# Attention over 400,000 sorted edges: 138 dense groups in place of 136, lookups five to a batch, counts five, four and then three, and later nodes counted in one block

## The chip, the cores and the metric

The kernel runs on one NeuronCore of a Trainium2 chip. Its engines are TensorE (PE, with its weight loads as PEld), VectorE (DVE), ScalarE (ACT), GpSimd (POOL) and SyncE (SP). The metric is the device time of one launch in microseconds (us); less is better. Before the change three runs gave 3430.93, 3432.67 and 3432.46 us, a median of 3432.46 us.

## The reference

One graph-attention layer with a residual and a layer norm. There are 12,500 nodes with 64 features, 400,000 edges with 64 features of their own, and the edges are sorted by destination:

```python
h_src = nfeats[src]; h_dst = nfeats[dst]
e = leaky_relu(concat([h_src, h_dst, efeats]) @ W_attn + b_attn, 0.01)[:, 0]
m = concat([h_src, efeats]) @ W_ne
alpha = exp(e - segment_max(e, dst)[dst]); alpha /= segment_sum(alpha, dst)[dst]
z = segment_sum(alpha[:, None] * m, dst)
out = relu(concat([nfeats, z]) @ W_out)
x = layernorm(x + out, eps=1e-5)
```

Destinations are drawn as 12500·u², so the first nodes have very many edges and the last ones few.

## The kernel before, in words

**Groups.** The edges are cut into 782 groups of 512 (128 partitions times T = 4). A group covers a window of neighbouring destination nodes: a few nodes at the start of the list, up to 48 at its end.

**Sparse groups and batches.** Groups 136 to 781 are done by gathering: for each group POOL issues four indirect DMAs (`gather`, L335), each of which fetches 128 rows of a table in HBM into a tile `zx`; SP fetches the edges' own rows into the same tile. A tile holds four groups, and there are ZB = 9 of them. Groups go in 42 batches of 16 (four tiles each); the last four batches have 10, 10, 12 and 6. For one batch DVE makes `scores` tile by tile (L370 to L388), then `softmax` (L669 on, starting with the transpose at L694) runs in five steps over partitions and lines with four small DMA round trips by ACT, then `weights` (L791), and PE multiplies weights by gathered rows (`products`, L808). Two of a batch's four tiles are multiplied at once, the other two (`later`) between the softmax steps of the next batch; only then is a `zx` tile free for a new gather. DVE adds the sums into a ring (`add_in`, L827).

**Dense groups.** The first 136 groups have so few nodes that nothing is gathered for them. *Lookups* find the source's score: ACT turns a row of source numbers into a 0/1 matrix (`look_turn`, L427 and L428, a buffer of the pool `big`), PE multiplies (L438), DVE picks (`look_scores`, L463 to L469), and `look_rows` (L448 to L457) adds the edges' own part for a whole batch. When all groups of a *round* (`ROUNDS`) are looked up, they take part in the softmax of the next batch that is free for it. *Counts* then sum the weights by source and node: for each of four columns ACT writes a 0/1 block (L477, L478, a `big` buffer each), DVE writes `lows` (L480), PE multiplies the two into a PSUM bank (L485), and DVE adds the bank into `counts` (`dense_sum`, L503). A block of 490 columns covers five nodes. For a sixth, seventh or eighth node there is one more `big` buffer each, with four Square operations of 98 columns (L490), one Relu (L491), four matmuls (L493) and one addition (L506).

**Chunks.** Groups whose nodes lie together form a chunk (`CHUNKS`). In the batch after a chunk's last count PE multiplies `counts` by all node features (`node_products`, L562, 50 records), DVE picks the result and clears `counts` (`node_pick`, L570 to L575). `edge_products` (L546) does the edges' part once per batch.

**The order.** All of this is one hand-written order: a Python loop emits, batch by batch and tile by tile, the instructions of every engine, and each engine runs its list in order. At the second tile of the next batch stand: its lookup (L427), the blocks of count 0 (L477), and then `between` (`far`, L635, and four more by ACT; `step`, L639, by DVE). At the third tile stand `look_rows` and count 1, at the fourth `ep` is loaded. In the softmax's steps stand counts 2 and 3 and the lookups after the second one. `dense_step` sums open counts in steps 0 and 3. The number of `big` buffers is BIG = 6.

**What a batch has.** `alike` takes up to four groups for the lookups of a batch and up to four for its counts, and stops at the ends of rounds, of node limits (`NODS`) and, for counts, of chunks. That gives lookups in batches 1 to 34, four each, and counts in batches 5 to 38, four each:

| counts per group | batches, before |
|---|---|
| 2 nodes | 5 to 8 |
| 3 nodes | 9 to 13 |
| 4 nodes | 14 to 19 |
| 5 nodes | 20 to 26 |
| 6 nodes | 27 to 31 |
| 7 nodes | 32 to 36 |
| 8 nodes | 37 and 38 |

A chunk ends in batches 13, 16, 19, 21, 23, 25 and in each of 26 to 38.

Of the kernel before, what the change touches and what calls it, by code (L numbers as in the profile page):

```python
# [9 lines left out]
F32 = mybir.dt.float32  # L10
# [5 lines left out]
P = 128  # L16
T = 4
# [10 lines left out]
BIG = 6  # L28
# [30 lines left out]
def sorted_path(ctx, tc, x, dst, idx, edge, w_ne, w_attn, b_attn, w_out, out, flag):  # L59
# [24 lines left out]
    ones_row = const.tile([1, P], F32, name="ones_row")  # L84
    nc.vector.memset(ones_row, 1.0)
# [3 lines left out]
    ENDS = ((3, 3, 2, 2), (3, 3, 2, 2), (3, 3, 3, 3), (2, 2, 1, 1))  # L89
# [25 lines left out]
    def each_of(g):  # L115
        return next(n for upto, n in EACHS if g < upto)

# [105 lines left out]
    sixth, seventh, eighth, probe = cut(pps, NB, NB, NB, 8)  # L223
    more_nodes, w_dst, w_src = (sixth, seventh, eighth), sixth[:, 0:D], seventh[:, 0:D]
# [18 lines left out]
    def dense_places(srcs, fit):  # L243

        assert max(n for _, n in NODS) <= FIT + len(more_nodes)
# [43 lines left out]
    def slots_of(k):  # L289

        g0, G = starts[k], sizes[k]
        drel = chunks.tile([P, T, BG], F32, name="drel", bufs=3)
# [69 lines left out]
    def scores(g0, n, zx, drel, b0, plain):  # L362
# [6 lines left out]
        pr = feats.tile([P, SG, T, D], F32, name="pr", bufs=1)  # L369
# [37 lines left out]
    def look_loads(g0, n):  # L407

        many = nodes_of(g0)
        wrow = tiny.tile([P, EACH, NOD], F32, name="wrow_d", bufs=1)[:, :, 0:many]  # L410
        nc.sync.dma_start(out=wrow[:, 0:n], in_=wins[g0 // P][g0 % P:g0 % P + n, 0:many].unsqueeze(0).to_broadcast([P, n, many]))
        return dense_edges(g0, n, "ed", True), wrow
# [28 lines left out]
    def look_rows(g0, n, loads):  # L441
# [4 lines left out]
        pr = feats.tile([P, SG, T, D], F32, name="pr", bufs=1)  # L446
# [12 lines left out]
    def look_scores(g, found):  # L459

        pr = feats.tile([P, SG, T, D], F32, name="pr", bufs=1)
# [9 lines left out]
    def dense_counts(g):  # L471
# [14 lines left out]
        for j in range(nodes_of(g) - FIT):  # L486
            at = wide + j * NB
            hi = big().rearrange("l p t -> l (p t)")[:, 0:T * NB].rearrange("l (t h) -> l t h", t=T)
            for t in range(T):
                nc.scalar.activation(hi[:, t], places[:, at:at + NB], AF.Square, bias=place[:, t, g:g + 1])  # L490
            nc.scalar.activation(hi, hi, AF.Relu, scale=-1.0, bias=1.0)  # L491
            for t in range(T):
                nc.tensor.matmul(more_nodes[j], lows[t], hi[:, t], start=(t == 0), stop=(t == T - 1), skip_group_check=True)  # L493
        return g, to

    def dense_sum(g, to):
# [69 lines left out]
    def node_pick(g0, pairs):  # L566

        pr = feats.tile([P, SG, T, D], F32, name="pr", bufs=1)
# [62 lines left out]
    def between(k):  # L631
# [17 lines left out]
    def at_ends(step, same, pen, mask):  # L649
# [6 lines left out]
    def lines_of(step, same, pen, mask):  # L656
# [4 lines left out]
        return step, same, pen, mask, rw  # L661

    def softmax(k, about, carry, d=None, carry_d=None):
# [8 lines left out]
        step, same, pen, mask = about[0:4]  # L672
# [29 lines left out]
        to_lines(ends_of, bnd)  # L702
        yield
        in_lines()
        rw = about[4]
# [173 lines left out]
    with before:  # L879
# [23 lines left out]
        with tc.manual_schedule(engines={EngineType.DVE, EngineType.Pool, EngineType.Activation, EngineType.PE, EngineType.SP}):  # L903
# [27 lines left out]
            nc.vector.tensor_copy(edge_both, pwt[:, 2, 0:D])  # L931
            d0f = pre.tile([1, NG], F32, name="d0f", bufs=1)
# [131 lines left out]
    def centred(c0, po):  # L1064
# [15 lines left out]
        sq = feats.tile([P, SG, T, D], F32, name="pr", bufs=1)[:, 0]  # L1080
# [6 lines left out]
    def scaled(c0, yo, sq, var, more=False):  # L1087
# [3 lines left out]
        if more:  # L1091
            nc.scalar.activation(scrap_row[:, 0:1], ones_row[:, 0:1], AF.Exp)
# [23 lines left out]
    with loop:  # L1116
# [38 lines left out]
        def alike(todo, ends_=chunk_ends):  # L1155
# [676 lines left out]
```

## Time and profile before

The profiled execution took 3432.35 us; its span, from the first to the last instruction, is 3430.6 us.

| engine | busy us | share of the span | instructions |
|---|---|---|---|
| PE | 2334.8 | 68% | 10444 |
| DVE | 2232.5 | 65% | 5723 |
| ACT | 1382.4 | 40% | 3178 |
| POOL | 2454.1 | 72% | 2614 |

How to read it: no engine is busy all the time, and the shares are means over a kernel whose stages differ. A useful mark is the transpose at L694, which DVE does once per batch, when all scores of the batch are there. In this document *stretch k* runs from that mark of batch k to that of batch k+1. It holds the softmax and the weights of batch k, the scores of batch k+1, the softmax-time lookups and counts of batch k, and the first lookups and counts of batch k+1. Stretch 26 begins 2186.8 us after the span's start, stretch 37 at 3145.8, stretch 41 at 3391.2.

### The profile page before, as it was taken

The numbers are of one execution on the slowest core, as the hardware profiler recorded it, in microseconds if no ns is written. First come the engines' busy times: TensorE is split into PE (matmuls) and PEld (weight loads), VectorE is DVE, ScalarE is ACT, GpSimd is POOL, SyncE is SP. The second block draws the span as 40 slices with busy tenths as digits, with TensorE's granted clock in tenths as the row PEclk, the third lists the DMA queues.
The fourth block names the chain that finished last, engine by engine and source line by source line (L and its number), as shares of the span: only waits on it lengthen the run. The fifth ranks groups of instructions, "written<-read, shape, count | busy, mean of one in ns | idle before, by whom it ended". The sixth has DMA issues, their size and how long they took to land. (4 is left out here: it accounts for less than half of the span.)

```text
span 3430.6 us, 40536 instructions
## 1 busy us (share of the span) xinstructions
PE 2334.8 (68%) x10444; PEld 1953.5 (57%) x10444; DVE 2232.5 (65%) x5723; ACT 1382.4 (40%) x3178; POOL 2454.1 (72%) x2614
## 2 busy tenths in 40 slices
PE   0244445666667676765777787788888788888864
PEld 0244445565566565664666565666666666666653
DVE  5654455666666667666676767767777667675565
ACT  0111123433333434344344544445554555565632
POOL 6777777777777777777777777777777776774460
PEclk9999996555555566666666676677777777777865
DMA  9433334334444434343343434344344333332230
GB/s 128 88 67 67 66 73 76 75 74 79 84 77 80 89 63 94 74 76 76 75 79 74 76 76 91 76 77 77 74 80 76 67 71 74 63 65 53 43 68 11
DMA packets 821663, 253.18 MB, mean 74 GB/s; under 512 B 740890, under 2 KB 780009, under 8 KB 821426
## 3 DMA queue, kind: packets, MB, share of 16 engines
q1 hardware_dynamic: 697356, 163.64, 24.2%
q0 software_dynamic: 82912, 86.20, 14.7%
q10 hardware_dynamic: 41158, 0.66, 0.7%
q8 instruction: 90, 1.47, 0.2%
q14 instruction: 147, 1.20, 0.1%
HBM read 243.18 MB, written 6.80 MB: 73 GB/s over the span
## 5 line engine op out<-in xcount | busy, mean ns | idle before, releaser
L335 POOL DMA_INDIRECT zx<-table,srcs x2520 | 2383.5, 946 | 869.8 <-issue 702.3
L808 PE MATMUL pg<-w,zx 128*128 128x40 f32 (+9 forms) x5024 | 983.0, 366 | 165.4 <-DMA zx<-table,srcs 99.5
L808 PEld LDWEIGHTS pg<-w,zx 128*128 128x128 f32 x5024 | 962.7, 297 | 182.7 <-issue 99.6
L485 PE MATMUL pg<-big,lows 128*128 128x490 f32 (+3 forms) x1088 | 582.9, 700 | 381.2 <-DVE lows L480 325.4
L485 PEld LDWEIGHTS pg<-big,lows 128*128 128x128 f32 x1088 | 282.7, 274 | 623.6 <-issue 430.1
L438 PE MATMUL pg<-s_src,big 128*128 128x98 f32 x1088 | 291.3, 445 | 302.0 <-DVE pr L465 162.9
L438 PEld LDWEIGHTS pg<-s_src,big 128*128 128x128 f32 x1088 | 266.1, 328 | 305.3 <-issue 171.7
L477 ACT ACTIVATE big<-places,place 128x490 f32<-128x490 int16 (+3 forms) x544 | 338.5, 622 | 80.0 <-PE pg L438 56.1
L478 ACT ACTIVATE big<-big 128x490 f32<-128x490 f32 (+3 forms) x544 | 296.3, 545 | 17.3
L372 DVE TENSOR_REDUCE fixed<-pr 128x16 f32<-128x1024 f32 (+2 forms) x168 | 199.3, 1186 | 155.6 <-ACT fixed L368 146.4
L377 DVE TENSOR_TENSOR fixed<-fixed,zx 128x16 f32<-128x16 f32 (+2 forms) x168 | 30.9, 184 | 360.5 <-DMA zx<-table,srcs 356.4
L562 PE MATMUL pg<-xall,counts 128*128 128x256 f32 x950 | 243.1, 421 | 3.5 <-DVE yo L1079 3.3
L562 PEld LDWEIGHTS pg<-xall,counts 128*128 128x128 f32 x950 | 201.0, 215 | 42.7 <-issue 9.8
L370 DVE TENSOR_TENSOR pr<-zx,lines 128x1024 f32<-128x1024 f32 (+2 forms) x168 | 197.0, 1173 | 4.8 <-DMA zx<-in_edge_dram 4.4
L368 ACT ACTIVATE fixed<-wrow 128x80 f32<-128x80 f32 (+9 forms) x168 | 44.6, 265 | 354.8 <-DVE lows L480 130.1
L480 DVE TENSOR_SCALAR lows<-fixed,low,kept 128x128 f32<-128x128 f32 x544 | 185.3, 401 | 2.5 <-PE pg L485 2.5
L696 ACT ACTIVATE soft<-turned 128x128 f32<-128x128 f32 x42 | 16.3, 389 | 414.0 <-DVE turned L694 414.0
L427 ACT ACTIVATE big<-low_of,p_col 128x512 f32<-128x512 bf16 x136 | 98.0, 720 | 186.6 <-DMA low_of<-low_rows 141.6
L827 DVE TENSOR_TENSOR acc<-acc,pg 128x28 f32 (+9 forms) x646 | 120.2, 186 | 69.2 <-issue 21.9
L490 ACT ACTIVATE big<-places,place 128x98 f32<-128x98 int16 x336 | 97.7, 362 | 70.3 <-PE pg L438 52.5
L803 PE MATMUL pg<-zx,ident 1*1 1x32 f32 (+2 forms) x336 | 41.2, 207 | 123.5 <-issue 115.1
L379 DVE TENSOR_TENSOR hot<-fixed,drel 128x320 bf16<-128x320 f32 (+9 forms) x168 | 107.8, 642 | 6.0 <-issue 0.2
(400 smaller groups left out, 2703.0 us busy)
## 6 DMA issues: line engine op xcount, KB each, us to landing
zx<-in_edge_dram SPq DMA_DIRECT2D x645, 128.0 KB
zx<-table,srcs POOLq DMA_INDIRECT x2520
ed<-in_edge_dram SPq DMA_DIRECT2D x34, 512.0 KB
low_of<-low_rows SPq DMA_DIRECT2D x136, 128.0 KB
ep<-in_edge_dram SPq DMA_DIRECT2D x136, 128.0 KB
table<-xall SPq DMA_DIRECT2D x7, 455.0 KB
out_dram<-yo SPq DMA_DIRECT2D x24, 128.0 KB
xall<-in_x_dram SPq DMA_DIRECT2D x13, 224.0 KB
```

Source lines behind the costliest of these rows:

```text
L335: nc.gpsimd.indirect_dma_start(out=zx[0:r, g, t, 1:EW] if plain else zx[0:r, g, t, 0:EW], out_offset=None, in_=x[:, :] if plain else table ...
L370: nc.vector.tensor_tensor(pr[0:r, 0:n], ze[0:r, 0:n], w_edge[0:r].unsqueeze(1).to_broadcast([r, n, T, D]), op=OP.mult)
L372: nc.vector.tensor_reduce(ysum[0:r, 0:n], pr[0:r, 0:n], axis=AX.X, op=OP.add)
L379: nc.vector.tensor_tensor(hot[0:r, 0:n], slots[0:r, 0:Sk].unsqueeze(1).unsqueeze(1).to_broadcast([r, n, T, Sk]), drel[0:r, :, b:b + n].rea ...
L438: nc.tensor.matmul(found[:, t, :], hot[:, :, t], s_src, start=True, stop=True)
L477: nc.scalar.activation(hi, places[:, 0:wide], AF.Square, bias=place[:, t, g:g + 1])
L478: nc.scalar.activation(hi, hi, AF.Relu, scale=-1.0, bias=1.0)
L480: nc.vector.tensor_scalar(lows[t], count_, low[:, t, g:g + 1], kept[:, t, kept_at(g):kept_at(g) + 1], op0=OP.is_equal, op1=OP.mult)
L485: nc.tensor.matmul(to, lows[t], highs[t], start=(t == 0), stop=(t == T - 1))
L562: nc.tensor.matmul(pairs[0:m * ND, 0:m * D], counts[:, h0:h0 + m, :].rearrange("l h n -> l (h n)"), xall[:, h0:h0 + m, 1:EW], start=(h0 == ...
L808: nc.tensor.matmul(pg[:, g, :], zx[:, g, t, 1:EW + D], w[:, g, t, :], start=(t == 0), stop=(t == T - 1)).ins
L827: nc.vector.tensor_tensor(ag, ag, pg[:, g, :], op=OP.add)
```

## The change

- **More dense groups.** 138 in place of 136. The last two batches have 11 and 5 groups (12 and 6 before); the batches of 16 and the two of 10 stay. Two groups are eight gathers.
- **A new plan.** Rounds of 5, 10, 15, 15, 15, 10, 10, 12, 12, 13, 12 and 9 groups; the lookups are taken up to five to a batch, the counts up to five (groups 0 to 79), four (80 to 107) and three (from 108 on). There are 21 chunks in place of 19. No group has more than seven nodes.
- **A fifth count.** A batch with five counts has its third one at the fourth tile, ahead of that tile's scores, and the two open ones are summed first.
- **A fifth lookup** is picked after the softmax.
- **Sixth and seventh nodes in one block**: Squares of 196 columns for two of the four columns per buffer, matmuls of 196 columns, one addition.
- **Memory.** BIG goes from 6 to 5. `pr`, `ed`, `ep` and two small tiles hold five groups. The `mask` of the softmax is made by ACT behind the first DMA of the softmax, in one buffer, and no longer in `between`. Two small tiles go or shrink.

| counts per group | batches, after |
|---|---|
| five of 2 nodes | 3, 5, 6 |
| five of 3 nodes | 8 to 11 |
| five of 4 nodes | 12 to 16 |
| five of 5 nodes | 17 to 20 |
| four of 5 nodes | 21 and 22 |
| four of 6 nodes | 23 to 27 |
| three of 7 nodes | 28 to 37 |

Lookups stand in batches 1 to 30, five each but for 18 and 22 (three and two), 19, 23, 25 and 30 (four) and 28 (two). A chunk ends in batches 11, 14, 16, 18 to 27, 29 and 31 to 37.

```diff
-BIG = 6
+BIG = 5
-ROUNDS = (12, 12, 12, 12, 12, 12, 12, 12, 12, 12, 8, 8)
+ROUNDS = (5, 10, 15, 15, 15, 10, 10, 12, 12, 13, 12, 9)
-EACHS = ((136, 4),)
-EACH = max(n for _, n in EACHS)
-CHUNKS = ((36, 1), (12, 2), (8, 3), (4, 13))
-NODS = ((16, 2), (36, 3), (60, 4), (88, 5), (108, 6), (128, 7), (136, 8))
+LOOKS = ((138, 5),)
+EACHS = ((80, 5), (108, 4), (138, 3))
+EACH = max(n for _, n in LOOKS + EACHS)
+CHUNKS = ((35, 1), (15, 1), (10, 2), (5, 2), (4, 7), (6, 2), (3, 6))
+NODS = ((15, 2), (35, 3), (60, 4), (88, 5), (108, 6), (138, 7))
-    ENDS = ((3, 3, 2, 2), (3, 3, 2, 2), (3, 3, 3, 3), (2, 2, 1, 1))
+    ENDS = ((3, 3, 2, 2), (3, 3, 2, 2), (3, 3, 3, 2), (2, 1, 1, 1))
...
-        for j in range(nodes_of(g) - FIT):
-            at = wide + j * NB
-            hi = big().rearrange("l p t -> l (p t)")[:, 0:T * NB].rearrange("l (t h) -> l t h", t=T)
-            for t in range(T):
-                nc.scalar.activation(hi[:, t], places[:, at:at + NB], AF.Square, bias=place[:, t, g:g + 1])
+        more = max(0, nodes_of(g) - FIT) * NB
+        for t0 in range(0, T if more else 0, 512 // max(more, P)):
+            ts = range(t0, min(t0 + 512 // max(more, P), T))
+            hi = big().rearrange("l p t -> l (p t)")[:, 0:len(ts) * more].rearrange("l (t h) -> l t h", h=more)
+            for i, t in enumerate(ts):
+                nc.scalar.activation(hi[:, i], places[:, wide:wide + more], AF.Square, bias=place[:, t, g:g + 1])
             nc.scalar.activation(hi, hi, AF.Relu, scale=-1.0, bias=1.0)
...
-        for j in range(nodes_of(g) - FIT):
-            at = counts[:, :, ds(vs[0] + FIT + j, 1)]
-            nc.vector.tensor_tensor(at, at, more_nodes[j].unsqueeze(2), op=OP.add)
+        more = nodes_of(g) - FIT
+        if more > 0:
+            at = counts[:, :, ds(vs[0] + FIT, more)]
+            nc.vector.tensor_tensor(at, at, more_nodes[:, 0:more * NB].rearrange("p (j h) -> p h j", h=NB), op=OP.add)
...
-        mask = rows.tile([P, 2, P], F32, name="mask", bufs=2)
-        nc.scalar.activation(mask, pen, AF.Relu, bias=1.0)
-        return step, same, pen, mask
+        return step, same, pen
...
         to_lines(ends_of, bnd)
+        mask = rows.tile([P, 2, P], F32, name="mask", bufs=1)
+        nc.scalar.activation(mask, pen, AF.Relu, bias=1.0)
...
-                    batch_looks = alike(looks, ())
+                    batch_looks = alike(looks, (), look_of)
...
+                    if i == 3 and len(batch_counts) > 4:
+                        while open_counts:
+                            dense_sum(*open_counts.pop(0))
+                        open_counts.append(dense_counts(batch_counts[2]))
                     hot = scores(g0, n, tiles[i], drel, b0, k == 0)
...
-                assert not seen and (not final or not open_counts)
+                while seen:
+                    look_scores(*seen.pop(0))
+                assert not final or not open_counts
```

How the order moves, at three places.

First DVE, at the fourth tile of a batch with counts of five nodes. Before, from the end of `look_rows` (L457) to the first operations of the tile's scores (L370):

```order
L457 TENSOR_TENSOR y_dense<-total 128x4x4
L480 TENSOR_SCALAR lows<-fixed,low,kept 128x128 x4
L370 TENSOR_TENSOR pr<-zx,lines 128x1024
L372 TENSOR_REDUCE fixed<-pr 128x16
L377 TENSOR_TENSOR fixed<-fixed,zx 128x16
```

In the change, batch 20:

```order
L462 TENSOR_TENSOR y_dense<-total 128x4x4
L485 TENSOR_SCALAR lows<-fixed,low,kept 128x128 x4
L504 TENSOR_LOAD rel
L509 ISA
L509 TENSOR_TENSOR counts<-counts,pg 128x98x5
L504 TENSOR_LOAD rel
L509 ISA
L509 TENSOR_TENSOR counts<-counts,pg 128x98x5
L485 TENSOR_SCALAR lows<-fixed,low,kept 128x128 x4
L372 TENSOR_TENSOR pr<-zx,lines 128x1024
L374 TENSOR_REDUCE fixed<-pr 128x16
```

Two sums and four more `lows` now stand ahead of the tile's scores; the second sum needs PE's product of count 1, whose `lows` stand just above it.

Second ACT, at the second tile, with the buffers' numbers (each `big` number is one use of a buffer). Before, batch 24, from the second lookup of the batch to `far`:

```order
L427 ACTIVATE big_14293<-low_of_14241,p_col_108 128x512
L428 ACTIVATE big_14293<-big_14293 128x512
L477 ACTIVATE big_14302<-places_110,place_114 128x490
L478 ACTIVATE big_14302<-big_14302 128x490
L477 ACTIVATE big_14307<-places_110,place_114 128x490
L478 ACTIVATE big_14307<-big_14307 128x490
L477 ACTIVATE big_14312<-places_110,place_114 128x490
L478 ACTIVATE big_14312<-big_14312 128x490
L477 ACTIVATE big_14317<-places_110,place_114 128x490
L478 ACTIVATE big_14317<-big_14317 128x490
L287 ACTIVATE lines_149<-srcs_14118 128x64
L635 ACTIVATE far_14328<-edges_of1_76 128x130
```

In the change, batch 20:

```order
L432 ACTIVATE big_12790<-low_of_12739,p_col_106 128x512
L433 ACTIVATE big_12790<-big_12790 128x512
L482 ACTIVATE big_12799<-places_108,place_112 128x490
L483 ACTIVATE big_12799<-big_12799 128x490
L482 ACTIVATE big_12804<-places_108,place_112 128x490
L483 ACTIVATE big_12804<-big_12804 128x490
L482 ACTIVATE big_12809<-places_108,place_112 128x490
L483 ACTIVATE big_12809<-big_12809 128x490
L482 ACTIVATE big_12814<-places_108,place_112 128x490
L483 ACTIVATE big_12814<-big_12814 128x490
L289 ACTIVATE lines_147<-srcs_12617 128x64
L642 ACTIVATE far_12825<-edges_of1_74 128x130
```

The rows are the same. With the batch's first lookup, which still holds a buffer, they use six; there were six, and now there are five, so the fourth block (`big_12814`) takes the buffer of the first lookup and waits until PE has multiplied it (L438, in the change L443).

Third ACT, in a count of seven nodes, the blocks of the sixth and seventh. Before:

```order
L477 ACTIVATE big<-places,place 128x490
L478 ACTIVATE big<-big 128x490
L490 ACTIVATE big<-places,place 128x98 x4
L491 ACTIVATE big<-big 128x392
L490 ACTIVATE big<-places,place 128x98 x4
L491 ACTIVATE big<-big 128x392
```

In the change:

```order
L482 ACTIVATE big<-places,place 128x490
L483 ACTIVATE big<-big 128x490
L496 ACTIVATE big<-places,place 128x196 x2
L497 ACTIVATE big<-big 128x392
L496 ACTIVATE big<-places,place 128x196 x2
L497 ACTIVATE big<-big 128x392
```

Two buffers as before, with four wider Squares in place of eight.

More of the change, by code (lines that the diff above doesn't have):

```diff
@@ L116, in each_of, with look_of @@
         return next(n for upto, n in EACHS if g < upto)
+    def look_of(g):
+        return next(n for upto, n in LOOKS if g < upto)
     def round_of(g):
@@ L243, in dense_places @@
     def dense_places(srcs, fit):
-        assert max(n for _, n in NODS) <= FIT + len(more_nodes)
+        assert max(n for _, n in NODS) <= FIT + 3
         ids_ = srcs[:, :, 0:T].rearrange("p g t -> p t g")
@@ L410, in look_loads @@
         wrow = tiny.tile([P, EACH, NOD], F32, name="wrow_d", bufs=1)[:, :, 0:many]
-        nc.sync.dma_start(out=wrow[:, 0:n], in_=wins[g0 // P][g0 % P:g0 % P + n, 0:many].unsqueeze(0).to_broadcast([P, n, many]))
+        for k in range(g0 // P, (g0 + n - 1) // P + 1):
+            a, b = max(g0, k * P), min(g0 + n, (k + 1) * P)
+            nc.sync.dma_start(out=wrow[:, a - g0:b - g0],
+                              in_=wins[k][a - k * P:b - k * P, 0:many].unsqueeze(0).to_broadcast([P, b - a, many]))
         return dense_edges(g0, n, "ed", True), wrow
@@ L485, in dense_counts @@
             nc.tensor.matmul(to, lows[t], highs[t], start=(t == 0), stop=(t == T - 1))
[L486 to L490 removed]
+        more = max(0, nodes_of(g) - FIT) * NB
[4 more added lines that the diff above has]
+                nc.scalar.activation(hi[:, i], places[:, wide:wide + more], AF.Square, bias=place[:, t, g:g + 1])
             nc.scalar.activation(hi, hi, AF.Relu, scale=-1.0, bias=1.0)
[L492 to L493 removed]
+            for i, t in enumerate(ts):
+                nc.tensor.matmul(more_nodes[:, 0:more], lows[t], hi[:, i], start=(t == 0), stop=(t == T - 1), skip_group_check=True)
         return g, to
@@ L566, in node_pick @@
     def node_pick(g0, pairs):
-        pr = feats.tile([P, SG, T, D], F32, name="pr", bufs=1)
+        pr = feats.tile([P, EACH, T, D], F32, name="pr", bufs=1)
         mine = pr[:, 0]
@@ L644, in between, with at_ends @@
         nc.scalar.activation(pen[:, 1, :], far[:, 1:P + 1], AF.Identity, bias=nfar)
-        mask = rows.tile([P, 2, P], F32, name="mask", bufs=2)
-        nc.scalar.activation(mask, pen, AF.Relu, bias=1.0)
-        return step, same, pen, mask
-    def at_ends(step, same, pen, mask):
+        return step, same, pen
+    def at_ends(step, same, pen):
         outer_ = rows.tile([P, 2], F32, name="outer_", bufs=2)
@@ L654, in at_ends, with lines_of @@
         to_lines(pens_of, outer_)
-    def lines_of(step, same, pen, mask):
+    def lines_of(step, same, pen):
         rw = tiny.tile([1, 4, P], F32, name="rw", bufs=1)
@@ L660, in lines_of @@
         nc.scalar.activation(as_pairs(rw[:, 2:4, :]), in_order(pens_of), AF.Relu, bias=1.0)
-        return step, same, pen, mask, rw
+        return step, same, pen, rw
     def softmax(k, about, carry, d=None, carry_d=None):
@@ L671, in softmax @@
         assert d is None or G == BS
-        step, same, pen, mask = about[0:4]
+        step, same, pen = about[0:3]
         flat_m = mrow.rearrange("o k i -> o (k i)")
@@ L931, in sorted_path @@
             nc.vector.tensor_copy(edge_both, pwt[:, 2, 0:D])
+            ones_row = pre.tile([1, P], F32, name="ones_row", bufs=1)
+            nc.vector.memset(ones_row, 1.0)
             d0f = pre.tile([1, NG], F32, name="d0f", bufs=1)
@@ L1153, in sorted_path, with alike @@
         loads = rows_again = None
-        def alike(todo, ends_=chunk_ends):
+        def alike(todo, ends_=chunk_ends, each=each_of):
             n = 0
-            while n < min(each_of(todo[0]) if todo else 0, len(todo)) and not (n and todo[n] in edges_) and not (n and todo[n] in ends_):
+            while n < min(each(todo[0]) if todo else 0, len(todo)) and not (n and todo[n] in edges_) and not (n and todo[n] in ends_):
                 n += 1
```

22 lines of the change are left out of this document (10 added, 12 removed).

## The prediction

> **What bounds the kernel now.** I read the waits of POOL first, then stretches of 100 us, then the waits of DVE, then the stretches between the softmax marks. POOL's waits from 100 to 2800 us (first row) and from there on (second), and two stretches of 100 us (us, then busy time and count of PE, PEld, DVE, ACT, POOL):
>
> ```profile
> POOL zx L335 <- issue: 604.5, 1984, 0.3
> ...
> POOL zx L335 <- PE pg L808: 88.0, 8, 27.2
> ...
> 300.00:400.00 100.00, 53.88 (x248) 52.04 (x248) 45.97 (x121) 19.94 (x51) 75.61 (x81) 1.00 0.42 80
> 1900.00:2000.00 100.00, 80.44 (x329) 64.31 (x328) 76.52 (x201) 49.73 (x104) 75.70 (x80) 0.65 0.51 100
> ```
>
> Up to 2800 us POOL issues a gather every 1.24 us, whatever the others do: that is the pace, 64 gathers or 79.9 us per batch of 16. Then it waits 88 us for tiles that PE has not yet multiplied: there the rest of the kernel is behind POOL. DVE's waits up to 2187 us (first row) and after:
>
> ```profile
> DVE fixed L377 <- DMA zx<-table,srcs: 356.4, 49, 12.5
> ...
> DVE dens L740 <- ACT lines L599: 83.1, 16, 8.9
> DVE step L639 <- ACT far L635: 68.4, 11, 11.7
> ```
>
> DVE waits 356 us for gathered rows before 2187 us, and after it never notably: stretch 26 is the first that is longer than the pace, and from there to the end the time is the sum of what each stretch needs for itself. I call that its own length; before 2187 us it is the length less the wait at L377. The late stretches:
>
> ```profile
> 2186.80:2270.60 83.80, 70.64 (x278) 56.73 (x279) 57.71 (x140) 36.74 (x77) 63.39 (x68) 0.69 0.40 77
> 2270.60:2355.80 85.20, 71.42 (x318) 56.05 (x317) 61.67 (x149) 44.38 (x96) 64.48 (x69) 0.74 0.40 77
> 2355.80:2444.50 88.70, 71.81 (x320) 57.04 (x318) 63.85 (x157) 45.02 (x99) 67.07 (x72) 0.73 0.40 75
> 2444.50:2530.10 85.60, 72.84 (x320) 58.61 (x318) 63.11 (x150) 44.12 (x94) 64.58 (x70) 0.72 0.40 77
> 2530.10:2612.40 82.30, 68.22 (x304) 53.17 (x303) 60.07 (x141) 40.30 (x89) 62.30 (x66) 0.75 0.42 78
> 2703.70:2796.40 92.70, 75.00 (x348) 60.56 (x348) 64.55 (x154) 50.39 (x114) 70.15 (x75) 0.74 0.39 74
> ...
> 2974.30:3052.50 78.20, 67.11 (x316) 53.70 (x316) 54.96 (x132) 45.57 (x109) 55.36 (x59) 0.77 0.37 67
> 3052.50:3145.80 93.30, 76.06 (x332) 60.60 (x332) 56.61 (x144) 50.04 (x124) 54.04 (x58) 0.71 0.30 54
> 3145.80:3230.10 84.30, 70.90 (x348) 56.25 (x348) 50.17 (x141) 51.38 (x126) 37.75 (x40) 0.80 0.24 43
> 3230.10:3295.40 65.30, 52.47 (x252) 42.52 (x252) 41.67 (x114) 27.93 (x73) 35.24 (x38) 0.75 0.25 44
> 3295.40:3352.50 57.10, 34.66 (x162) 32.29 (x163) 36.53 (x98) 16.00 (x38) 39.10 (x42) 0.50 0.32 61
> 3352.50:3391.20 38.70, 16.31 (x180) 13.96 (x179) 24.93 (x75) 9.21 (x28) 0.86 (x1) 0.50 0.07 11
> 3391.20:3430.60 39.40, 12.37 (x168) 11.26 (x168) 18.32 (x75) 7.23 (x18) 0.00 (x0) 0.50 0.06 12
> ```
>
> These are stretches 26 to 30, 32 and 35 to 41. At pace stretch 37 would begin at 2186.8 + 11 x 79.9 = 3065.7 us; it begins at 3145.8, a *lag* of 80 us. So the eight gathers that go (10 us of POOL) are worth nothing by themselves. The change is worth what it does to the lag and to stretches 37 to 41.
>
> **What a lookup and a count cost.** Groups of stretch 23 (five nodes, four lookups and counts; busy us, mean ns), a pick's longest operation in stretch 26, and the page's row for a block of a sixth node:
>
> ```profile
> L480 DVE TENSOR_SCALAR lows<-fixed,low,kept 128x128 f32<-128x128 f32 x16 | 5.5, 402 | 1.2 <-PE pg L485 1.2
> L503 DVE TENSOR_TENSOR counts<-counts,pg 128x490 f32 x4 | 2.7, 664 | 0.8 <-issue 0.7
> L465 DVE TENSOR_TENSOR pr<-pr,pg 128x392 f32<-128x392 f32 x4 | 2.2, 562 | 0.3
> L448 DVE TENSOR_TENSOR pr<-ed,lines 128x1024 f32<-128x1024 f32 x1 | 1.2, 1208 | 0.0
> L384 DVE TENSOR_TENSOR pr<-hot,fixed 128x512 f32<-128x512 bf16 x4 | 2.7, 686 | 0.1
> ...
> L485 PE MATMUL pg<-big,lows 128*128 128x490 f32 x32 | 17.3, 699 | 2.7 <-DVE lows L480 2.7
> ...
> L575 DVE MEMSET counts<- 128x3136 f32 x1 | 2.7, 2672 | 0.6 <-issue 0.6
> ...
> L490 ACT ACTIVATE big<-places,place 128x98 f32<-128x98 int16 x336 | 97.7, 362 | 70.3 <-PE pg L438 52.5
> ```
>
> A lookup costs DVE three operations like L465 and a short one, 1.9 us, and in `look_rows` a quarter of two like L448, 0.6 us: 2.5. A count costs it 1.4 (L480), 0.7 (L503) and some 0.5 of short ones: 2.5. The third of five counts also makes DVE wait for PE at the fourth tile: at least 0, at most the group's products (17.3 / 4 = 4.3 us) less the 2.1 that DVE does meanwhile; I take 1.2, between the two. So a fifth lookup and count are 6.2 us a batch. A pick is 2.7 and two short operations, 3.7. Four window columns less save about 0.09 us in each of four operations like L384 on four tiles: 1.3. The `mask` that ACT makes later falls into its wait for the softmax's first DMA, and the smaller tiles move no instruction of the loop: nothing, or at most one ACT operation like L490 a batch, 0.4 us, if that cover is gone. A fifth lookup's and count's work on ACT and PE lies beside DVE's, as that of the four does.
>
> **Five buffers.** Stretch 23 is one with `node_products`. ACT, PE and DVE there, its whole row, DVE's wait for gathered rows in it and in stretch 20, and DVE's wait at `step` in stretch 26:
>
> ```profile
> 1997.31 0.30 ACT L635 ACTIVATE far<-edges_of 128x130 f32<-128x130 int32 x1
> 2009.96 0.70 ACT L477 ACTIVATE big<-places,place 128x490 f32<-128x490 int16 x1 [9.81 <-PE pg L438]
> ...
> 1993.73 12.38 PE L562 MATMUL pg<-xall,counts 128*128 128x256 f32 x50
> 2007.84 2.08 PE L438 MATMUL pg<-s_src,big 128*128 128x98 f32 x8
> ...
> 1998.31 0.28 DVE L639 CUSTOM_DVE_ANT_0 step<-far 128x129 f32<-128x129 f32 x1
> ...
> 1947.40:2026.80 79.40, 63.12 (x257) 50.23 (x256) 53.08 (x136) 33.55 (x67) 59.91 (x65) 0.72 0.41 79
> ...
> DVE fixed L377 <- DMA zx<-table,srcs: 10.5, 2, 7.3
> DVE fixed L377 <- DMA zx<-table,srcs: 3.4, 1, 3.4
> ...
> DVE step L639 <- ACT far L635: 11.7, 1, 11.7
> ```
>
> With six buffers ACT does all of count 0 and `far`, and only then waits for PE's lookup (2009.96). With five the fourth block of count 0 takes that wait, and `far` comes behind it, at 2009.9 + 1.3 = 2011.2 in place of 1997.3; `step` on DVE is ready at 1998.3 and now waits 13 us. Behind `step` in DVE's list stand the scores of the third and fourth tile, and so the next softmax. The bounds are 0 (DVE there later, or PE earlier) and 13; from stretch 26 on, where a sixth node needs one buffer more, the wait is already there, 68.4 us over 11 times, and 11.7 in stretch 26. So stretch 23 would need 79.4 - 10.5 = 68.9, plus 13 less 2 of other waits that go: 80. Plus a pick it is 83.7, and stretch 26, which is that, took 83.8.
>
> **The sum, stretch by stretch**, own length against the pace of 79.9.
>
> - *3 to 13*, two to four nodes: 68 to 84 by the steps below; what lag arises is caught up within two stretches. Lag 0.
> - *14 to 20*, five lookups and five counts. Chunk ends 14, 16 and 18: 80 + 6.2 = 86. 19 and 20 have a pick too: 89 and 87 (the batch after 20 has four counts). 15 and 17, without `node_products`, from stretch 20 as it was (80.0 - 3.4 + 6.2, less 1.3): 81 and 82. Together 597 against 559: lag 38.
> - *21 and 22*, four counts of five nodes, some lookups less: 83.5 and 81.5. Lag 43.
> - *23 to 27*, four counts of six nodes, from the mean of 27 to 30 as they were, 85.4: plus 1.9 to 2.5 for a fifth lookup in most, 1.3 for the fourth block behind PE's lookup, -1.3 for narrower windows, 3 for the joined round in 26 (as stretch 28 has it). In 27 -5.3, since the batch after it has no count at its third tile (a count 2.5, its later nodes 0.7, and 2.0 of wait at L372 of the fourth tile, the first row below). 86, 87.4, 86, 91, 81: lag 75.
> - *28 to 30*, three counts of seven nodes, from 92.7: -5.3; -2 for the merged blocks (ACT's eight times 0.36 become four times about 0.45, between the rows of 98 and 490 columns, and DVE has an addition less in three groups); no `node_products` in 28 and 30 (68.4 / 11 = 6.2 of wait less); lookups as planned. 76, 84, 77: lag 72.
> - *31 to 36*, no lookups, from 78.2 (stretch 35): -5.3, -2, and plus 4.3, since seven nodes need six buffers of five, as eight nodes need seven of six in stretch 37 now, which then waits this (second row):
>
> ```profile
> DVE fixed L372 <- ACT fixed L368: 4.4, 3, 2.0
> ...
> DVE step L639 <- ACT far L635: 4.3, 1, 4.3
> ```
>
>   That is 75; 71.5 in 31 without a pick; 86 in 34 from 93.3 with the last round. 457.5 against 479.4: lag 50. Stretch 37 begins at 3065.7 + 50 = 3116.
> - *37*, from 84.3: no counts beside the scores, the wait above gone, a node less: 62. *38*: what stretch 39 does now, with two of twelve groups less: 53. *39*: no dense work, between 38.7 (stretch 40, six groups to score) and 57.1 (with a pick, block 0 and a group more): 46, near the middle, since it scores eleven groups. *40 and 41*: a group less, 37 and 39.
>
> The end is 3116 + 237 = 3353 us of span. The execution is 1.75 us longer than its span (3432.35 against 3430.6) and agrees with the median of the runs, 3432.46: **3355 us**, 2.3% less.
>
> **Rivals.** *No lag left.* If the 13 us of wait for `far` does not come, since DVE is later at `step` in five-count batches, stretches 14 to 27 lose most of their 75, and stretch 37 begins at pace: 3065.7 + 237 + 2 = 3305 us. For it: 79.4 - 53.1 = 26 us of DVE idle in stretch 23. Against: stretch 26.
>
> *Slower.* Five buffers hold ACT back at other places too: count 1 and 2 take turns with the second lookup's buffer, held until the softmax, so ACT writes blocks no faster than PE frees them, and DVE's window copies (L368) stand behind. For it: ACT already waits 70.3 us before L490. Price: 4 us in each of stretches 14 to 36 gives 23 x 4 = 92, 3447 us; it decides from 3.6 us a stretch on. The Trainium skill (Perfetto Trace Analysis, Optimization Strategy) says that one gap repeated over a stretch can mean too few buffers; the L639 row with its 11 waits agrees, and that speaks for this rival.
>
> *No change.* The same with a little less, 3.3 us a stretch, would end at 3431.
>
> *POOL's pace slips* under more DVE work. 81 gathers per 100 us at 46 us of DVE, 80 at 76.5: if one in 80 is lost from stretch 3 on to 20, 18 us, and the lag hides it: 3355 to 3373, inside the forecast's range. The Trainium skill (SBUF — State Buffer, section "SBUF: two separate sides") states that a VectorE operation on two ports keeps GpSimd from writing descriptors; the two rows show at most this 1%.
>
> **How the numbers follow.** Own lengths good to 1.5 us over 23 stretches give the forecast 3325 to 3395: chance 0.60. No lag left, below 3325: 0.15. Between 3395 and 3425: 0.05. No change: 0.06. Slower: 0.14. The range of 8 in 10 is 3303 to 3430. About 0.2%, 7 us, is what a measurement tells from no change: faster 0.80, same 0.06, slower 0.14.
>
> **What would show it.** Right: DVE's wait at `far` of 6 to 13 us from stretch 14 on; waits for gathered rows gone there; stretch 37 near 3116; no mark later than before from 37 on; POOL's wait of 88 us below 60. Wrong: marks of stretches 20 to 30 over 80 us behind pace, or `far` not waited for.

## The result and the profile after

The changed kernel takes 3389.9 us, median of four runs (3385.84 to 3392.76), where the kernel before takes 3431.69: a ratio of 0.9878, 95% interval 0.9861 to 0.9895. That is 42 us less; 3355 was predicted, 77 less. The profiled execution takes 3388.03 us with a span of 3386.3.

The changed kernel leaves something out. In batches 12, 15, 17, 19 and 20, which have five counts and follow a chunk's end, the first two counts are added into `counts` at the fourth tile, and only then does the pick in the softmax clear `counts` (around stretch 12: sums at 1061.7 and 1065.4 us, the clearing at 1075.5). So 10 of the 138 groups are missing from the node sums. Every instruction still runs, but the 42 us are the gain of an order that loses these sums; what a mended order takes is asked in e12.

The same four parts of the span, first of the kernel before, then of the changed one: stretches 1 to 10, 11 to 29, 30 to 36, and 37 to the end. The columns are us, then busy time and count of PE, PEld, DVE, ACT and POOL, the granted clock, the DMA share and GB/s:

```profile
186.80:986.90 800.10, 446.67 (x1990) 415.80 (x1990) 455.94 (x1239) 230.98 (x588) 604.97 (x641) 0.75 0.40 75
986.90:2530.10 1543.20, 1163.19 (x4872) 946.08 (x4872) 1068.67 (x2708) 681.47 (x1462) 1166.78 (x1236) 0.67 0.41 78
2530.10:3145.80 615.70, 503.20 (x2323) 403.77 (x2321) 428.55 (x1035) 333.87 (x776) 432.67 (x458) 0.75 0.37 69
3145.80:3430.60 284.80, 186.71 (x1108) 156.27 (x1108) 171.62 (x497) 111.75 (x282) 112.95 (x120) 0.65 0.21 38
```

```profile
186.70:986.20 799.50, 489.47 (x2158) 449.68 (x2158) 497.57 (x1347) 272.21 (x671) 604.25 (x641) 0.66 0.41 80
986.20:2627.60 1641.40, 1291.50 (x5358) 1031.80 (x5358) 1126.73 (x2850) 759.89 (x1600) 1190.43 (x1261) 0.70 0.39 76
2627.60:3153.80 526.20, 390.43 (x1804) 306.95 (x1804) 359.84 (x860) 246.51 (x545) 393.71 (x418) 0.73 0.38 68
3153.80:3386.30 232.50, 132.96 (x810) 116.73 (x810) 147.40 (x432) 69.26 (x174) 119.61 (x127) 0.57 0.25 44
```

The end is 52.3 us shorter (284.8 to 232.5), stretches 30 to 36 are 89.5 shorter, and the middle, 11 to 29, is 98.2 longer: 1641.4 us for 19 stretches, whose pace by POOL is 19 x 79.9 = 1518. DVE is busy only 58 us more in the middle, so 40 of the 98 are added waiting. At stretch 37 the marks stand at 3153.8, 8 us later than before, and not at the predicted 3116.

DVE's longest waits in the changed kernel over the whole span (us in total, times, longest):

```profile
DVE step L646 <- ACT far L642: 219.3, 32, 16.5
DVE fixed L379 <- DMA zx<-table,srcs: 151.2, 25, 11.9
DVE fixed L374 <- ACT fixed L370: 83.3, 34, 26.9
DVE counts L509 <- PE pg L490: 65.1, 26, 4.8
```

And POOL's for tiles that PE still holds, over the whole span and from 2800 us on:

```profile
POOL zx L337 <- PE pg L815: 71.4, 13, 15.0
...
POOL zx L337 <- PE pg L815: 1.6, 1, 1.6
```

`step` waits 219 us for `far`: the wait that was predicted to come with the fifth buffer, and larger than its price. Waits for gathered rows (L379) fall from 356 to 151 us, and there is none after stretch 10: from stretch 11 on POOL no longer sets the time. POOL's wait for PE, nearly all of it after 2800 us before, now lies ahead of that.

Stretch 19 of the changed kernel (1663.1 to 1754.7 us, five nodes, after a chunk's end) on PE, ACT and DVE:

```profile
1713.06 12.41 PE L569 MATMUL pg<-xall,counts 128*128 128x256 f32 x50
1725.39 2.40 PE L553 MATMUL pg<-wd,ep 128*128 128x10 f32 x20
1727.65 2.08 PE L443 MATMUL pg<-s_src,big 128*128 128x98 f32 x8
...
1729.77 0.70 ACT L482 ACTIVATE big<-places,place 128x490 f32<-128x490 int16 x1 [15.45 <-PE pg L443]
1731.22 0.29 ACT L642 ACTIVATE far<-edges_of 128x130 f32<-128x130 int32 x1
...
1731.55 0.30 DVE L646 CUSTOM_DVE_ANT_0 step<-far 128x129 f32<-128x129 f32 x1 [15.17 <-ACT far L642]
```

PE works through the 50 node products (12.4 us), the edge products and the lookup's products; only then does ACT get the buffer for the fourth block of count 0, having stood still for 15.45 us; `far` comes 1.5 us behind it, and `step` has waited 15.17.

### The profile page after: what moved, and what is told of

Its sections match the earlier page's. It is cut to its first block, busy times and chain, and to the rows that moved or that the text cites. A ratio compares the mean times of both kernels' runs of the same rounds, so it can differ in the third digit from the quotient of the medians.

```text
span 3386.3 us, 40132 instructions
## 1 busy us (share of the span) xinstructions
PE 2339.4 (69%) x10284; PEld 1936.7 (57%) x10284; DVE 2240.6 (66%) x5741; ACT 1371.3 (40%) x3058; POOL 2445.2 (72%) x2604
## 3 DMA queue, kind: packets, MB, share of 16 engines
q0 software_dynamic: 82656, 85.93, 14.8%
## 5 line engine op out<-in xcount | busy, mean ns | idle before, releaser
L815 PE MATMUL pg<-w,zx 128*128 128x40 f32 (+9 forms) x5024 | 973.1, 364 | 208.7 <-DVE w L798 106.5
L815 PEld LDWEIGHTS pg<-w,zx 128*128 128x128 f32 x5024 | 953.1, 295 | 225.6 <-DVE w L798 110.7
L490 PE MATMUL pg<-big,lows 128*128 128x490 f32 (+3 forms) x1104 | 580.7, 684 | 309.3 <-DVE lows L485 260.0
L490 PEld LDWEIGHTS pg<-big,lows 128*128 128x128 f32 x1104 | 273.6, 264 | 559.1 <-issue 370.2
L443 PE MATMUL pg<-s_src,big 128*128 128x98 f32 x1104 | 295.8, 439 | 155.0 <-ACT big L433 113.1
L443 PEld LDWEIGHTS pg<-s_src,big 128*128 128x128 f32 x1104 | 269.6, 329 | 167.9 <-ACT big L433 161.4
L569 PE MATMUL pg<-xall,counts 128*128 128x256 f32 (+1 forms) x1050 | 271.8, 424 | 0.7 <-DVE yo L1088 0.6
L374 DVE TENSOR_REDUCE fixed<-pr 128x16 f32<-128x1024 f32 (+3 forms) x168 | 198.8, 1183 | 97.1 <-ACT fixed L370 83.3
L569 PEld LDWEIGHTS pg<-xall,counts 128*128 128x128 f32 (+1 forms) x1050 | 224.2, 218 | 44.7 <-issue 7.0
L372 DVE TENSOR_TENSOR pr<-zx,lines 128x1024 f32<-128x1024 f32 (+3 forms) x168 | 196.9, 1172 | 6.0 <-DMA zx<-in_edge_dram 5.2
L370 ACT ACTIVATE fixed<-wrow 128x80 f32<-128x80 f32 (+9 forms) x168 | 44.4, 264 | 327.8 <-DVE w L798 125.4
L646 DVE CUSTOM_DVE_ANT_0 step<-far 128x129 f32<-128x129 f32 x42 | 12.3, 293 | 219.5 <-ACT far L642 219.3
L509 DVE TENSOR_TENSOR counts<-counts,pg 128x490 f32 (+3 forms) x138 | 81.3, 589 | 85.2 <-PE pg L490 65.1
L379 DVE TENSOR_TENSOR fixed<-fixed,zx 128x16 f32<-128x16 f32 (+3 forms) x168 | 31.0, 184 | 156.2 <-DMA zx<-table,srcs 151.2
L810 PE MATMUL pg<-zx,ident 1*1 1x32 f32 (+3 forms) x336 | 40.7, 205 | 107.3 <-DVE pr L470 59.1
```

What stands on the lines that cost most here:

```text
L372: nc.vector.tensor_tensor(pr[0:r, 0:n], ze[0:r, 0:n], w_edge[0:r].unsqueeze(1).to_broadcast([r, n, T, D]), op=OP.mult)
L374: nc.vector.tensor_reduce(ysum[0:r, 0:n], pr[0:r, 0:n], axis=AX.X, op=OP.add)
L443: nc.tensor.matmul(found[:, t, :], hot[:, :, t], s_src, start=True, stop=True)
L490: nc.tensor.matmul(to, lows[t], highs[t], start=(t == 0), stop=(t == T - 1))
L569: nc.tensor.matmul(pairs[0:m * ND, 0:m * D], counts[:, h0:h0 + m, :].rearrange("l h n -> l (h n)"), xall[:, h0:h0 + m, 1:EW], start=(h0 == ...
L815: nc.tensor.matmul(pg[:, g, :], zx[:, g, t, 1:EW + D], w[:, g, t, :], start=(t == 0), stop=(t == T - 1)).ins
```

## The experiments

I began with two theories. **A**: the lag of the middle is this wait, and the wait is the lost buffer. **B**: the lag is the work of five lookups and five counts; the wait only fills time that DVE would spend waiting elsewhere. Later came **C**: the wait is PE's order, the node products ahead of what ACT's blocks wait for, and five buffers only make more blocks wait on it.

The first four runs (e1 to e4) fell on a chip on which the kernel before takes 4791 us, the last one (e12) on another on which it takes 4775; the section on the hardware comes back to this. There the kernels are told by their ratio to the kernel before alone; the changed kernel itself was not run on either. Runs e5 to e11 fell on three more chips and stand beside a kernel before of 3435 to 3438 us, 3 to 6 us more than beside the changed kernel, so differences to its 3389.9 us are good to some us only.

**e1, five buffers alone.** Against the kernel before:

```diff
-BIG = 6
+BIG = 5
```

> The kernel before with five block buffers in place of six and nothing else changed. Theory A (the lag of the changed kernel is the wait of DVE's step for ACT's far, and that wait comes from the fifth buffer): the wait at step, 68 us over 11 times, grows to 130 to 200 us; stretches 13, 16, 19, 21 and 23 reach 77 to 81 us of own length and stay hidden behind POOL, 25 goes over the pace, and 26 to 34 get 1 to 4 us longer each: 3450 to 3475 us. Theory B (the lag comes from the work of five lookups and five counts, and the wait only fills time that DVE would spend waiting elsewhere): with four of each nothing moves, 3425 to 3440 us.

On that chip 5044.53 against 4790.93 us, ratio 1.0487 (1.0427 to 1.0547): the fifth buffer's loss costs, and more than it does in e9. Run again as e9 on a chip where the kernel before takes 3435 us:

> The kernel before with five block buffers and nothing else changed, on a chip where the kernel before takes its 3432 us. Theories A and C: the wait at step grows from 68 us to 150 to 220; up to stretch 24 it is hidden behind POOL, 25 passes the pace and 26 to 37 get 1 to 8 us longer each: 3450 to 3500 us. Theory B: 3425 to 3440 us.

3475.06 us, ratio 1.0115 (1.0091 to 1.0140). DVE's wait at `step` in e9:

```profile
DVE step L639 <- ACT far L635: 195.9, 34, 16.6
```

And its stretches 11 to 29 and 30 to 36, columns as above:

```profile
986.90:2543.80 1556.90, 1175.48 (x4876) 954.36 (x4876) 1069.91 (x2707) 682.51 (x1462) 1177.04 (x1247) 0.67 0.42 78
2543.80:3182.40 638.60, 518.79 (x2316) 413.36 (x2316) 428.84 (x1035) 334.62 (x776) 421.76 (x447) 0.73 0.36 66
```

With not one instruction of work added, the wait grows from 80 (all 20 times of the whole span) to 196 us, and the kernel loses 40 us. Nearly all of it falls after stretch 25, where POOL no longer hides it: stretches 26 to 36 take 1.5 to 5.4 us more each. Theory B does not stand for this part.

**e2 and e7, six buffers in the changed kernel.** Against the changed kernel:

```diff
-BIG = 5
+BIG = 6
...
-        yo = work.tile([P, NBC, D], F32, name="yo", bufs=2)
+        yo = work.tile([P, NBC, D], F32, name="yo", bufs=1)
```

> The changed kernel with six block buffers again; the room comes from the tile of an output block, one in place of two, which can cost 2 to 3 us at the very end. Theory A: for counts of up to five nodes the wait at far goes (stretches 11 to 21: about 85 us less), for six and seven nodes it falls to about 6 us in a stretch: lag under 20 us at stretch 21 and under 60 at stretch 30, 3315 to 3350 us. Theory B: 3375 to 3395 us, with the wait moved to other lines.

There 4737.16 us, ratio 0.9852 (0.9803 to 0.9900). As e7 on a chip where the kernel before takes 3437 us:

> The changed kernel with six block buffers again (an output block's tile is one in place of two, for the room; 2 to 3 us at the very end at most), on a chip where the kernel before takes its 3432 us. Theory A and C alike (the fifth buffer's loss makes the wait): no wait over 2 us at step in stretches 5 to 22, 6 to 9 us at six and seven nodes; lag under 15 us at stretch 23, under 50 at stretch 30, 3300 to 3345 us. Theory B: 3375 to 3395 us.

3306.2 us, ratio 0.9618 (0.9602 to 0.9634), 84 us less than the changed kernel's 3389.9. The wait at `step` in e7:

```profile
DVE step L646 <- ACT far L642: 65.7, 13, 14.4
```

And stretches 11 to 29 and 30 to 36:

```profile
987.40:2544.20 1556.80, 1263.90 (x5358) 1018.28 (x5358) 1126.58 (x2850) 758.48 (x1600) 1176.95 (x1247) 0.71 0.42 80
2544.20:3067.00 522.80, 393.05 (x1804) 309.35 (x1804) 359.25 (x860) 245.85 (x545) 395.42 (x419) 0.74 0.39 68
```

DVE does the same work in the middle as in the changed kernel (1126.6 and 1126.7 us) in 84.6 us less. Stretch 37 begins at 3067.0: POOL's pace, 3065.7, to within 1.3 us. The wait is gone up to five nodes; at six nodes it remains, 5 to 14.4 us, where I expected 6 to 9.

**e3, e4 and e5, the order on ACT and on PE.** e3 writes `far` and what follows from it ahead of the second tile's count; e4 moves the node products on PE behind the first lookup's products; e5 does both:

```diff
-                        if chunk_of is not None:
-                            opened = node_products(chunk_of)
...
                         seen.append((batch_looks[0], look_products(turns.pop(0), shared)))
+                    if i == 1 and chunk_of is not None:
+                        opened = node_products(chunk_of)
...
+                    if k and i == 1 and not final:
+                        after = between(k + 1)
                     if k and i in (1, 2):
...
-                        if k + 1 < len(sizes):
+                        if k + 1 < len(sizes) and after is None:
```

> The changed kernel with the copy far and what follows from it written ahead of the second tile's count, so that ACT does far before the block that waits for PE's lookup. Theory A: the wait at step falls from 219 us to under 45; with every such wait at 1.3 us the marks add up to 3296 us, and some of it comes back as a wait for the window copies, which still stand behind that block: 3300 to 3345 us. Theory B: all of it comes back, 3375 to 3395 us.

> The changed kernel with the 50 node products moved on PE from ahead of the first lookup's products to behind them; buffers as they are. Theory A with PE's order as the cause of the length of the wait: PE's lookup comes 12 us earlier in stretches that follow a chunk's end, the wait at step falls from 219 to under 90 us, and the pick comes later but well within its time: 3300 to 3345 us. If the wait has to do with the buffers alone and not with what stands ahead of the lookup on PE: the wait stays over 180 us and the time at 3380 to 3395.

On the chip of e1: e3 4856.56 us, 1.0126 (1.0070 to 1.0182); e4 4807.54 us, 1.0006 (0.9965 to 1.0046). Their times decide nothing here. The trace of e3 does show where the wait goes: `step` waits no more, but DVE then stands at L372 for a copy that ACT makes behind the held block (L289):

```profile
DVE pr L372 <- ACT lines L289: 812.4, 33, 42.8
```

> The changed kernel with both edits: far and what follows from it ahead of the second tile's count on ACT, and the node products behind the first lookup's products on PE. Theory A (the lag is the wait at step, and that comes from the block that waits for PE's lookup): no wait at step over 2 us in stretches 5 to 37, no wait for the window copies in its place, lag under 25 us at stretch 30, 3296 to 3325 us where the kernel before takes 3432. Theory B (the lag is the work of five lookups and counts): 3370 to 3395 us. On a chip where the kernel before takes some 4790 us, as in the four runs ahead of this one, neither can be read off the total; then the marks decide nothing and the run only says how far the edits carry there.

3375.57 us, ratio 0.9814 (0.9798 to 0.9831): 14 us below the change where I expected at least 65. The same here: `step` waits no more, but DVE's next instruction does, the first of the third tile's scores (e5, DVE's waits over the whole span):

```profile
DVE pr L372 <- ACT lines L289: 198.6, 39, 15.6
```

Stretch 24 of e5 (six nodes) on PE and ACT shows why:

```profile
2117.77 2.15 PE L443 MATMUL pg<-s_src,big 128*128 128x98 f32 x8
2119.71 13.04 PE L569 MATMUL pg<-xall,counts 128*128 128x256 f32 x50
2132.68 3.55 PE L490 MATMUL pg<-big,lows 128*128 128x490 f32 x8
...
2133.81 1.18 ACT L496 ACTIVATE big<-places,place 128x98 f32<-128x98 int16 x4 [8.72 <-PE pg L490]
2135.45 0.27 ACT L289 ACTIVATE lines<-srcs 128x64 f32<-128x64 int32 x1
```

ACT itself stands still, so whatever comes behind the block makes DVE wait: `far` before, now the copy of L289. And at six nodes the count needs a fifth block (L496), whose buffer comes free with the count's *own* first products (L490); these now stood behind the node products. Up to five nodes the edit did what it should (lag 27 us at stretch 23, where the changed kernel has 65, both counted from stretch 1); from 23 on the lag grew as before, by 58 us up to stretch 28 in both. Both of my theories were too coarse; from this came C.

**e6, the node products behind the first count.** Against the changed kernel, one edit:

```diff
                     if i == 0:
-                        if chunk_of is not None:
-                            opened = node_products(chunk_of)
                         if edges_of or batch_looks or chunk_of is not None:
...
                             open_counts.append(dense_counts(g))
+                    if i == 1 and chunk_of is not None:
+                        opened = node_products(chunk_of)
                     if i == 3 and batch_counts:
```

> The changed kernel with one edit: the 50 node products stand on PE behind the first count's products at the second tile, in place of ahead of the edge and lookup products. Theory C (ACT's last blocks of the first count, which with five buffers wait for PE's lookup and, at six and seven nodes, for the first count's own products, stand behind the node products; whatever comes behind these blocks on ACT, far or the window copies, then holds DVE up): the wait of DVE at the third tile falls to 5 us in stretches of five nodes and 7 of six and seven, against 8 to 16 in the changed kernel; lag under 30 us at stretch 23, under 70 at stretch 30, 3340 to 3365 us. Theory B (DVE's own work makes the lag): at 3375 to 3395 us as before this edit.

3301.92 us, ratio 0.9604 (0.9588 to 0.9621), 88 us less than the change and 38 below the range I gave: the lag is 10 us at stretch 23 and 36 at 30, and it is caught up by stretch 36, which I had not counted on. PE and ACT in stretch 19 of e6 (start, us, and idle before with its releaser):

```profile
1693.13 2.14 PE L443 MATMUL pg<-s_src,big 128*128 128x98 f32 x8
1695.07 5.20 PE L490 MATMUL pg<-big,lows 128*128 128x490 f32 x8
1700.11 10.88 PE L569 MATMUL pg<-xall,counts 128*128 128x256 f32 x50
...
1695.31 0.70 ACT L482 ACTIVATE big<-places,place 128x490 f32<-128x490 int16 x1 [5.33 <-PE pg L443]
```

The wait at `step` over the whole span of e6; then in stretches 11 to 29 alone, first in the changed kernel, then in e6 with the one wait that is new there:

```profile
DVE step L646 <- ACT far L642: 95.9, 29, 5.8
...
DVE step L646 <- ACT far L642: 173.3, 19, 16.5
...
DVE step L646 <- ACT far L642: 58.2, 16, 5.8
...
DVE counts L509 <- PE pg L569: 18.2, 5, 5.9
```

And stretches 11 to 29 and 30 to 36 of e6:

```profile
988.50:2541.50 1553.00, 1268.96 (x5353) 1029.64 (x5353) 1126.47 (x2850) 759.13 (x1600) 1174.01 (x1244) 0.69 0.42 80
2541.50:3067.50 526.00, 405.01 (x1812) 317.92 (x1811) 359.78 (x859) 246.49 (x545) 397.71 (x422) 0.71 0.40 68
```

ACT's stop falls from 15.45 to 5.33 us, the longest wait at `step` from 16.5 to 5.8. In stretches 11 to 29, with DVE's busy time unchanged (1126.7 and 1126.5 us), `step` waits 115 us less; some 27 come back at other waits, 18 of them at sums into `counts` that now wait for the node products, and the stretches are 88 us shorter. With five buffers as they are, the order alone gives back what the buffer gave. Stretch 37 begins at 3067.5, on POOL's pace. Theory C stands by its mechanism; the time it gave was too high.

**e8, the same edit in the kernel before.**

> The kernel before with the one edit of run e6: the 50 node products on PE behind the first count's products at the second tile. Theory C: in stretches 26 to 37, where six to eight nodes ask more buffers than the six there are, the wait at step falls from 68 us over 11 times to 35 to 45 us; nothing moves before stretch 26; 3385 to 3415 us. If POOL or DVE's work made these stretches: within 5 us of 3432.

3414.38 us, ratio 0.9934 (0.9915 to 0.9953): at the upper edge of what C gave. `step` waits 31.0 us in all, 3.4 at most. In stretches 26 to 37 it is 18.4 us, less than the 35 to 45 I gave, but waits for window copies (L372) grow by 17 us there, so the time falls no further than C gave. Stretch 37 begins 25 us earlier (3121.2); stretches 36 and 37 gave 9 of it back (97.0 and 89.7 us, where they took 93.3 and 84.3). So the wait was a cost of the kernel before too, though a small one.

**e10, one sum in place of two at the fourth tile.** Against the changed kernel:

```diff
                     if i == 3 and len(batch_counts) > 4:
-                        while open_counts:
-                            dense_sum(*open_counts.pop(0))
+                        dense_sum(*open_counts.pop(0))
```

> The changed kernel, where at the fourth tile of a batch of five counts only the oldest open count is added up ahead of the third count, in place of both open ones; the second is added in the softmax. The wait of DVE for the second count's products (65 us over 26 times, 2 to 6 us in each stretch from 11 to 19) is what I priced at 1.2 us a batch. If it is a cost of its own: it falls under 25 us, stretches 11 to 19 get 2 to 4 us shorter each, 3350 to 3375 us. If the products are late anyway and the wait comes back in the softmax or at step: 3383 to 3395 us.

3391.72 us, ratio 0.9870 (0.9850 to 0.9891): the same as the change. DVE's waits for counts and for window copies:

```profile
DVE counts L509 <- PE pg L490: 14.9, 11, 2.9
...
DVE fixed L374 <- ACT fixed L370: 115.7, 52, 28.5
```

The wait for the second count's products falls from 65 to 15 us, but DVE then waits for the window copies, 116 us in place of 83. By stretch 20 it is 8 us ahead of the change, at stretch 37 under 4, and the time is the same: at the end it is not a cost of its own. (This order leaves out five groups' sums, not ten.)

**e11, six buffers and the new order.**

> The changed kernel with both: six block buffers and the node products behind the first count's products. After either edit alone stretch 37 begins at 3067 us, which is POOL's pace to the microsecond, so if POOL is the bound again both together gain nothing over either: 3298 to 3307 us, with DVE's wait for gathered rows over 230 us where it was 161 and 222. If some lag of the middle stretches still counts at the end: under 3295 us.

3304.59 us, ratio 0.9615 (0.9596 to 0.9633): nothing over either edit alone. In the middle it keeps pace as neither did (1519.2 us against 1518 at pace), and DVE waits 266.9 us for gathered rows; stretch 37 begins at 3066.6. POOL is the bound again, and what is left, 236 us from there on, is the end's own length.

**e12, the pick ahead.** The sums that the changed kernel leaves out are left out in e2 to e7 and in e11 too. All instructions run there, so the runs compare like with like, but none of these times is that of an order that keeps every sum. e12 is e6 with the pick written ahead of the adding up at the fourth tile:

```diff
                     if i == 3 and len(batch_counts) > 4:
+                        if opened:
+                            opened, picked_ = node_pick(*opened), True
                         while open_counts:
...
-                    if n == 0 and opened:
+                    if n == 0 and opened and not picked_:
```

> The kernel of run e6, and in the five batches of five counts that follow a chunk's end (12, 15, 17, 19, 20) the pick of node sums, which clears the counts, is written ahead of the fourth tile's adding up of counts, in place of behind it in the softmax; so the two counts added there stay in the next chunk. The same instructions in another order. In the softmax the pick lay partly in DVE's waits for the softmax's DMAs; at the fourth tile it lies open: 4 to 7 us longer in five stretches, lag 20 to 35 us more at stretch 21. If POOL's pace takes it back by stretch 37, as the stretches after 31 (63 to 76 us each of own length) allow: 3300 to 3310 us. If the lag then reaches stretch 37: 3310 to 3335 us.

It fell on a chip where the kernel before takes 4775 us: 4804.44 us, ratio 1.0048 (1.0015 to 1.0082). What the mended order costs where the kernel before takes 3432 us stays open; my estimate of 3300 to 3335 us is not tested.

## Why the prediction was right, and where not

The sign, the mechanism and the end were right; one term was too small. By the prediction's own steps:

- **Stretches 37 to 41**: 237 us predicted, 232.5 measured. **30 to 36**: 77 + 457.5 = 534.5 predicted, 526.2 measured. Dropping the third-tile count, the merged blocks and three counts in place of four were together worth a little more than their price; the runs do not tell them apart.
- **Stretches 1 to 10**: POOL's pace does not slip, 799.5 us against 800.1 with 42 us more of DVE work. That rival falls.
- **Stretches 11 to 29**: lag 75 predicted, 123 measured, and this is the whole miss: 48 here less the 8 and 4.5 above; the span came out 33 us over the predicted 3353. It splits into 9 us in 11 to 13, 11 in 14 to 20, 26 in 23 to 27, and 2 elsewhere. The sum for 14 to 20 also takes five lookups for every batch, while the plan has three in batch 18 and four in 19. At 2.5 us each that is 7.5 too much, so what was missing there is nearer 18 than 11.

The step that failed is "Five buffers", by its size. DVE's waits in the changed kernel, first stretches 14 to 20, then 23 to 27:

```profile
DVE step L646 <- ACT far L642: 65.0, 7, 15.2
DVE counts L509 <- PE pg L490: 31.2, 11, 4.8
...
DVE step L646 <- ACT far L642: 56.2, 5, 15.7
...
DVE fixed L374 <- ACT fixed L370: 14.8, 8, 2.0
```

And in the kernel before, stretches 27 to 30, from whose mean I took 23 to 27:

```profile
DVE step L639 <- ACT far L635: 27.5, 4, 9.1
...
DVE fixed L372 <- ACT fixed L368: 7.8, 8, 1.9
```

I priced the wait at 11 us net where node products stand ahead, and at nothing elsewhere. In 14 to 20 the five stretches with node products wait 10.9 us on average (7.7 to 15.2), as priced, but the two without wait 5.3 each, for the lookup alone. At six nodes I put 1.3 us on a mean wait of 6.9, 41 us over five stretches; it was 56, since in 24 and 27, which no joined round touches, DVE needs some 7 us less for itself, is at `step` that much sooner, and waits 15.4 and 15.7. In stretch 11, which I had on pace, it is 16.5. My upper bound of 13 us did not hold either: 16.5 in 11, 15.2 in 19, 15.1 in 21. The third count's wait for PE was 4.5 us in a stretch where I took 1.2, but in e10 most of it comes back as waits nearby. Of the 26 us in 23 to 27, 15 are `step` and about 5 the window copies (14.8 over five stretches against 7.8 over four); the remaining 6 are not traced to a row.

Of the signs listed, two came true: no wait for gathered rows from 14 on, and POOL's wait of 88 us from 2800 us on, which fell to 1.6 (over the whole span only from 90 to 71, since POOL now waits earlier). The waits at `far` came in part: up to stretch 27 they are 7 to 16 us, where 6 to 13 were given, but 5.3 in 15 and 17. Marks are earlier than before from 38 on, not from 37. A sign against it came true as well, lags over 80 us from stretch 25 on: the mechanism was right, its price too low. That the time still lies inside the forecast of 3325 to 3395 us is in part luck: with stretches 30 to 41 as summed, and not 13 us shorter, it would be some 3403.

The rival "no lag left", 3305 us, is not what the change does, but what it does once the wait is taken away: 3302 (e6), 3306 (e7), 3305 (e11). The slower rival was half right: ACT, held, does hold up more than `far` (e5), but not with 4 us more in every stretch. The Trainium skill (Perfetto Trace Analysis, Optimization Strategy) says that one gap repeated over a stretch, on the engine that should be saturated, can mean too few buffers. e9 and e7 agree: the sixth buffer is worth 40 us in the kernel before and 84 in the changed one. e6 adds that the order ahead of the releasing instruction gives 88 us without it.

## What to carry to other kernels

When a buffer goes, look up which instruction now waits, what stands ahead of its releaser on the other engine, and what stands behind the waiter on its own; price the hold anew in each stretch by when the victim arrives, not by a mean. Moving the victim out of the way only passes the wait to the next one (e3, e5); moving the long piece of work behind the releaser removes most of it (e6), and here cost no memory. And when sums move ahead in an order, look up what clears their target behind them.

## What the runs showed of the hardware

On two of the chips used, that of e1 to e4 and that of e12, all kernels take some 40 to 45% longer, the kernel before too (4791 and 4775 us in place of 3432). A count's products on PE in stretch 2 of e2 there:

```profile
453.44 1.02 PE L490 MATMUL pg<-big,lows 128*128 128x196 f32 x2 [4.59 <-issue]
459.73 1.02 PE L490 MATMUL pg<-big,lows 128*128 128x196 f32 x2 [5.27 <-issue]
```

PE's longest waits without a visible releaser over the whole span of e1 there:

```profile
PE pg L562 <- issue: 327.8, 188, 2.9
PE pg L808 <- issue: 212.6, 79, 19.0
PE pg L485 <- issue: 90.7, 23, 10.8
```

And all of them in e9, the same kernel on a chip where the kernel before takes 3435 us:

```profile
PE pg L803 <- issue: 71.3, 19, 4.5
PE pg L808 <- issue: 0.5, 1, 0.5
```

PE stops for some 5 us between pairs of products, and for up to 19 us elsewhere, where the trace shows nothing that holds it back; in e9 the node products (L562) have no such wait at all. The cause is not in these traces. On the chip of e1 the fifth buffer's loss costs 4.9% and not 1.2%, and on that of e12 the changed kernel with the new order and the pick ahead is no faster than the kernel before. So what an edit is worth on one of these chips does not tell what it is worth on another.
